# Cross-attention with its mask and its normalisation bias carried in the last row of the keys

## The chip, the core and the metric

The kernel runs on one core of a Trainium2 chip. The core has five engines that run their own instruction streams in program order: TensorE (PE, matmuls, with its weight loads shown apart as PEld), VectorE (DVE), ScalarE (ACT), GpSimd (POOL) and SyncE (SP, which here only issues DMAs). They wait for each other through semaphores. The metric is the device time of one execution in microseconds (us), lower is better. Before the change it is 2433.44 us, the median of three runs from 2432.4 to 2435.29.

## What is computed

Four attention blocks follow each other on a batch of 8 sequences of 256 tokens with 128 features; a memory of 64 vectors with 64 features (`ctx_512`) feeds every cross-attention. Blocks L0, L1 and L3 have one layer each. Block L2 is six layers of a decoder, and takes most of the time:

```python
def step(t, p):                       # six times, with other weights
    tn = _ln(t, norm_g, norm_b)
    t = _mha(tn, tn, skv, sq, sow, sob, tgt_mask) + t      # self-attention, 256 x 256
    tn = _ln(t, norm_g, norm_b)
    t = _mha(src, tn, ckv, cq, cow, cob, src_mask) + t     # cross-attention, 256 x 64
    tn = _ln(t, pg, pb)
    t = t + (jax.nn.relu(tn @ w1 + b1) @ w2 + b2)

def _mha(s, t, kv_w, q_w, o_w, o_b, mask):                 # H = 16 heads of D = 64
    ...
    scores = jnp.einsum('bhqd,bhkd->bhqk', q, k) * D ** (-0.5)
    scores = jnp.where(mask[:, None] == 0, jnp.float32(-1000000000.0), scores)
    attn = jax.nn.softmax(scores, axis=-1)
```

`_ln` subtracts the mean of a token's 128 features, divides by the deviation, multiplies by `norm_g` and adds `norm_b`. The normalised features of a token therefore sum to zero before `norm_g` and `norm_b` come in. The change touches the cross-attention of these six layers, and the order of some steps that L0 shares with it.

## The kernel before

Everything stays on the chip between layers: `t` holds the 2048 tokens as 16 tiles of 128 tokens. A sequence `b` is two such tiles (`qt` = 0, 1). PSUM, where matmuls write, is one pool of four buffers (`two_banks`, tag "ps"), handed out in turn: a matmul that takes the fifth buffer in program order waits until the readers of the first are done.

The order of all work is written out by hand. `at(tick, phase, fn)` (L279) puts a step into a plan; at the end (L1271 to L1282) the steps are traced by tick and then by phase, and every compute engine is held to that order. SP is not. A tick is no fixed time, only a place in the order.

In a decoder layer, self-attention of sequence b begins at tick T0 + 4b, and its projections up to four ticks earlier. Cross-attention of sequence b begins at T_ca + 2b with T_ca = T0 + 32, so that one tick holds one tile of 128 tokens ("CA tile" 0 to 15 below); feed-forward of b follows seven ticks later; the next layer's self-attention projections begin at T_ca + 12. The last self-attention output steps of sequence 7 (`out_proj`, L966, and its addition into `t`, `add_out`, L977) stand at T_ca + 2, those of sequence 6 at T_ca - 2.

For cross-attention the query and key weights are multiplied together once per layer. `plan_ca_weights` (L1005) does so around tick T = T_ca - 6: `turned` and `fetched` transpose the weights by way of DRAM, `regrouped` (L1030, POOL, tick T + 1), then `folded("AT", ...)` (L1062, tick T + 2) makes the 1024 x 128 product `AT` and `folded("WVO", ...)` (L1063, tick T + 3) the product of value and output weights; each has 32 PE instructions and two ACT copies out of PSUM (L1052, L1054). `keys_both` (L1071, every fourth tick, at T_ca - 2, + 2, + 6, + 10) multiplies `AT` with the memory of two sequences, and four ACT copies (L1085) move the result out of PSUM as the keys.

The queries are the normalised tokens, made by `ahead` (L802): statistics on DVE (L808, L809), scale and shift per token on POOL (`scales`, L814 to L821), applied on ACT (L827), transposed on PE (L841), and multiplied by `norm_g` and shifted by `norm_b` per feature while ACT moves them out of PSUM (L843).

One CA tile then goes through the steps of `plan_weights_64` (L314), which L0 uses too:

- `scores`, tick n, phase 1, PE: 16 score matmuls of 128 x 32 by 128 x 256 (L341), and behind each four of them four bf16 matmuls of a 32-column `ones0` with the mask row (L348), which add -BIG to masked keys;
- `lower`, tick n, phase 2: ACT copies the scores to `e` (L357), DVE takes the maximum of each head (L359), POOL subtracts it (L360);
- `exps`, tick n, phase 8: ACT, exponential in place (L366);
- `divide`, tick n + 1, phase 2.4: DVE sums (L370) and inverts (L371), POOL multiplies (L372);
- `turn`, tick n + 2, phase 2.5: DVE transposes in blocks (L380);
- `sums`, tick n + 3, phase 3.0: PE multiplies with the values (L388), DVE adds the result into `t` (L1104).

So DVE's order in a tick is maximum of tile n, sum of tile n - 1, transposes of tile n - 2, and POOL's is subtraction of tile n, multiplication of tile n - 1. Behind them, in even ticks, come the statistics for one cross-attention and one feed-forward sequence (phase 6, DVE) and their `scales` (phase 8.4, POOL).

Of the kernel before, what the change touches and what calls it, by code (L numbers as in the profile page):

```python
# [27 lines left out]
def tile_xattn_stack(ctx: ExitStack, tc: tile.TileContext, io, out: bass.AP):  # L28
# [28 lines left out]
    def big(tag, bufs=4, shape=(P, 1024), dtype=F32):  # L57

        return heap.tile(list(shape), dtype, tag=tag, name=uniq(tag), bufs=bufs)
# [93 lines left out]

    norm_g = column("L2_norm_g")
    norm_b = column("L2_norm_b")
    pre_g = load_const("L2_pre_gT", [D, NL])
    pre_b = load_const("L2_pre_bT", [D, NL])
    ff_b1 = load_const("L2_ff_b1T", [P, NL, FF // P])
# [88 lines left out]
        return nm  # L247


    nm2 = const.tile([P, B, M], BF16, tag="nm2", name="nm2")  # L250
    nc.vector.memset(nm2, 0.0)
    ones0 = const.tile([P, 32], BF16, tag="ones0", name="ones0")
    nc.vector.memset(ones0, 0.0)
    nc.vector.memset(ones0[0:1], 1.0)


    def stats(xin, eps):
# [53 lines left out]
        )  # L311
        return vw

    def plan_weights_64(tick, qt, qT, keys, values, mask, take):  # L314

# [1 line left out]

        def scores():  # L320
            sc = two_banks("sc").rearrange("p (q x) -> p q x", q=4)
            if mask is None:
                for i in range(4):
                    for a in range(4):
                        q = (i + 2 * (a // 2)) % 4
                        rows = slice(64 * (a // 2), 64 * (a // 2) + 64)
                        qb = 4 * qt + q
                        nc.tensor.matmul(
                            sc[32 * a : 32 * a + 32, q, :],
                            lhsT=qT()[rows, qb * 32 : (qb + 1) * 32],  # L330
                            rhs=keys()[rows, 4 * (a % 2) : 4 * (a % 2) + 4, :].rearrange(
                                "p h k -> p (h k)"
                            ),
                            start=True, stop=True,
                        )
                tl["sc"] = sc.rearrange("p q x -> p (q x)")
                return
            for q in range(4):
                qb = 4 * qt + q
                for a in range(4):  # L340
                    nc.tensor.matmul(  # L341
                        sc[32 * a : 32 * a + 32, q, :],
                        lhsT=qT()[:, qb * 32 : (qb + 1) * 32],
                        rhs=keys()[:, a].rearrange("p h k -> p (h k)"),
                        start=True, stop=False,
                    )
                for a in range(4):
                    nc.tensor.matmul(  # L348
                        sc[32 * a : 32 * a + 32, q, :], lhsT=ones0, rhs=mask,
                        start=False, stop=True,  # L350
                    )
            tl["sc"] = sc.rearrange("p q x -> p (q x)")

# [21 lines left out]

        def turn():
            e = tl.pop("e").rearrange("p (q h) (k x) -> p (h k) q x", q=4, x=32)
            eT = big("k" if mask is None else "o", shape=(P, 8, 4, 32))
            for i in range(2):
                nc.vector.transpose(eT[:, 4 * i : 4 * i + 4], e[:, 4 * i : 4 * i + 4])  # L380
            tl["eT"] = eT
# [12 lines left out]
        at(tick, 1, scores)  # L394
        at(tick, 2, lower)
        at(tick, 8, exps)
        at(tick + 1, 2.4, divide)
        at(tick + 2, 2.5, turn)
        at(tick + 3, 3.0, sums)


# [210 lines left out]

    def mask_keys():
        mi = big("q", dtype=I32)
        mi = mi[0:1, : B * M].rearrange("p (b m) -> p b m", b=B)
        nc.sync.dma_start(out=mi, in_=io["mask_Bx1xS2_if1"].rearrange("b o m -> o b m"))
        nc.vector.tensor_scalar(nm2[0:1], mi, 0.0, -BIG, ALU.is_equal, ALU.mult)

    mask_bf = []

# [41 lines left out]
    def plan_l0(b, T):  # L662
# [68 lines left out]
        at(T + 2, 3.2, make_values)  # L731
        for qt in range(QT):
            plan_weights_64(
                T + qt, qt, lambda: st["q"], lambda: st["k"], lambda: st["VW"], None,
                lambda ps, qt=qt: add(qt, ps),
            )
        at(T + 4, 6, moments)
# [267 lines left out]
    def plan_ca_weights(l, T):  # L1005
# [54 lines left out]
            at(T - 4 + i, -0.5, lambda i=i: fetched(i))  # L1060
        at(T + 1, 8.05, regrouped)
        at(T + 2, 3.6, folded("AT", 0, lambda c: st[1][:, :, c, :], HD ** -0.5))  # L1062
        at(T + 3, 3.6, folded("WVO", 1, lambda c: W["ca", l][2][:, c, :]))  # L1063

    keys_of = {}

    def plan_ca(l, b, T):
# [3 lines left out]
        def keys_both():  # L1071

            res = [big("q", shape=(D, 4, 4, M)) for _ in range(2)]
            for g in range(2):
# [7 lines left out]
                            start=True, stop=True,  # L1082
                        )
                for i in range(2):
                    nc.scalar.copy(  # L1085
                        res[i][:, :, 2 * g : 2 * g + 2, :].rearrange("p a r k -> p r a k"),
                        ps[:, :, :, i * M : (i + 1) * M],
                    )
            keys_of[b], keys_of[b + 1] = res

# [3 lines left out]
        def res():  # L1094
            st["tb"] = residual(b, W["ca", l][3])

        ahead(b, (T - 4, 6), (T - 3, 2.95), (T - 2, 2.9), norm_g, norm_b, st)
        if b % 2 == 0:
            at(T - 2, 3.7, keys_both)
        at(T + 2, 3.2, make_values)  # L1100
# [5 lines left out]
        for qt in range(QT):  # L1106
            plan_weights_64(
                T + qt, qt, lambda: st["tT"], lambda: keys_of[b], lambda: st["VW"],
                nm2[:, b].unsqueeze(1).to_broadcast([P, 4, M]), lambda ps, qt=qt: add(qt, ps),
            )  # L1110

    def plan_ff(l, b, T, T_second, steps=None):
# [117 lines left out]
    for l in range(NL):  # L1230
        T_ca = T0 + 4 * B
        T_next = T_ca + 2 * B
        for b in range(B):
            plan_sa(l, b, T0 + 4 * b)
        plan_ca_weights(l, T_ca - 6)
        for b in range(B):
            plan_ca(l, b, T_ca + 2 * b)
            T_ff = T_ca + 2 * b + 7
# [101 lines left out]
```

## Time and profile before

The profiled execution took 2433.93 us in all, and its span, from the first to the last instruction, is 2431.9 us. All times below are from this one execution, counted from the span's start.

| engine | busy us | share of the span | instructions |
|---|---|---|---|
| PE matmuls | 2349.5 | 97% | 42411 |
| PE weight loads | 1741.0 | 72% | 42411 |
| DVE | 1836.6 | 76% | 5988 |
| ACT | 1719.9 | 71% | 4528 |
| POOL | 1450.3 | 60% | 2483 |

The matmul count is twice the program's for most lines, because an f32 matmul leaves two records. A matmul's record is longer than the time it keeps PE from the next one (the records of one line overlap), so busy time over a line tells how long something of it was under way, not what its removal would free. The six cross-attention stages start (first record of L341) at 399.9, 771.4, 1144.3, 1516.1, 1888.2 and 2259.4 us, about 372 us apart, and the sixteen score blocks of the first stage at 399.9, 402.6, 409.5, 418.8, 423.1, 428.6, 432.9, 445.2, 451.2, 457.0, 464.8, 473.7, 483.9, 495.0, 504.5 and 511.8 us.

The groups of the table by line that the change touches, with count, busy us over all, and mean ns of one: the mask matmuls L348, 1536, 112.8, 274; the score matmuls L341, 3072, 218.6, 384; the key copies L1085 on ACT, 96, 49.3, 599; the maximum L359, 112, 136.8, 1221; the sum L370, 112, 135.3, 1208; POOL's subtraction L360 and multiplication L372, 112 each, 213.1 and 213.0, 1903 and 1902.

### The profile page before, as it was taken

To read this page: it belongs to the slowest core of one execution; us is meant where nothing else is said; L and a number is where in the kernel's file an instruction comes from. 1 tells how busy PE (TensorE), PEld (TensorE's weight loads), DVE (VectorE), ACT (ScalarE), POOL (GpSimd) and SP (SyncE) were. 2 spreads that over 40 slices of the span, in tenths; PEclk is the share of its full clock that TensorE was granted. 3 is DMA by queue.
4 is the path that set the end of the run, shared out by engine and by line. 5 is a ranking of instruction groups with operands and counts; after the bars stand their busy time and mean duration, and the time that the engine had idled before them with its cause. 6 is when DMAs were issued, how large, how long until landed. Compare 5 with 4: busy or idle time off the path is not lost.

```text
span 2431.9 us, 99981 instructions
## 1 busy us (share of the span) xinstructions
PE 2349.5 (97%) x42411; PEld 1741.0 (72%) x42411; DVE 1836.6 (76%) x5988; ACT 1719.9 (71%) x4528; POOL 1450.3 (60%) x2483
## 2 busy tenths in 40 slices
PE   8999999999999999999999999999999999999997
PEld 4667777677777777777777777777777777777675
DVE  4778887667888667888667888667888667888674
ACT  4567777667777667777667778567778657778662
POOL 3754556755556755556765556765555765555774
PEclk9999999999999999999999999999999999999998
DMA  6000022001022001012000012000013000011000
GB/s 178 2 2 20 20 72 65 2 3 30 20 64 73 3 3 30 20 55 73 12 2 26 23 52 77 12 2 18 25 43 85 21 2 18 25 28 39 2 4 16
DMA packets 102833, 76.87 MB, mean 32 GB/s; under 512 B 8114, under 2 KB 96882, under 8 KB 102387
## 3 DMA queue, kind: packets, MB, share of 16 engines
q1 hardware_dynamic: 101794, 70.16, 10.4%
q8 instruction: 333, 5.46, 1.0%
q14 instruction: 114, 0.93, 0.1%
q10 hardware_dynamic: 592, 0.33, 0.1%
HBM read 62.07 MB, written 8.39 MB: 29 GB/s over the span
## 4 chain that ended last, share of the span: by engine, by line
PE 79%; DVE 7%; ACT 7%; POOL 5%; issue 2%; DMA 0%; SPq 0%; POOLq 0%; DVEq 0%; ACTq 0%
PE mm L861 14%; PE sc L898 14%; PE mm L953 13%; PE mm L971 7%; PE mm L880 7%; PE mm L388 5%; PE sc L341 4%; PE mm L1137 3%; PE mm L1120 3%; DVE m L359 2%; ACT e L357 2%; POOL e L360 2%; PE mm L303 1%; PE tp L841 1%; PE mm L1079 1%
## 5 line engine op out<-in xcount | busy, mean ns | idle before, releaser
L927 POOL TENSOR_SCALAR e<-e,rs 128x256 f32<-128x256 f32 x1536 | 703.1, 478 | 674.9 <-DVE rs L925 665.6
L917 ACT ACTIVATE e<-e,mn 128x256 f32<-128x256 f32 x1536 | 758.2, 495 | 133.7 <-DVE mn L912 129.4
L912 DVE CUSTOM_DVE_ANT_0 e<-sc,nm 128x256 f32<-128x256 f32 x1536 | 542.5, 419 | 108.8 <-PE sc L898 106.2
L937 DVE STREAM_TRANSPOSE eTc<-e 128x512 f32<-128x512 f32 x768 | 517.3, 695 | 62.9 <-POOL e L927 61.6
L898 PE MATMUL sc<-k,q 64*32 64x256 f32 x12288 | 378.3, 380 | 1.9 <-ACT q L867 0.9
L953 PE MATMUL mm<-eTc,v 32*64 32x256 f32 x12288 | 363.7, 378 | 5.7 <-ACT AT L1054 3.3
L953 PEld LDWEIGHTS mm<-eTc,v 32*64 32x64 f32 x12288 | 276.8, 131 | 89.1 <-issue 22.4
L360 POOL TENSOR_TENSOR e<-e,m 128x1024 f32<-128x1024 f32 x112 | 213.1, 1903 | 208.4 <-DVE m L359 208.4
L359 DVE TENSOR_REDUCE m<-sc 128x16 f32<-128x1024 f32 x112 | 136.8, 1221 | 263.8 <-ACT e L357 263.8
L898 PEld LDWEIGHTS sc<-k,q 64*32 64x32 f32 x12288 | 220.9, 106 | 123.3 <-issue 49.6
L917 ACT ACTIVATION_READ_ACCUMULATOR e<-e,mn 128x1 f32 x1536 | 287.2, 187 | 0.0
L341 PE MATMUL sc<-q,tT 128*32 128x256 f32 x3072 | 218.6, 384 | 2.3 <-DVE t L1104 2.3
L372 POOL TENSOR_TENSOR e<-e,r 128x1024 f32<-128x1024 f32 x112 | 213.0, 1902 | 1.2 <-DVE r L371 1.2
L388 PE MATMUL mm<-v,o 128*128 128x128 f32 x1536 | 199.3, 285 | 0.2 <-ACT v L309 0.2
L388 PEld LDWEIGHTS mm<-v,o 128*128 128x128 f32 x1536 | 185.6, 198 | 15.9 <-issue 8.1
L861 PE MATMUL mm<-tT,w_sk 128*128 128x256 f32 x768 | 189.1, 389 | 0.0
L971 PEld LDWEIGHTS mm<-w_sow,o 128*128 128x128 f32 x1536 | 175.1, 192 | 16.2 <-issue 12.3
L880 PE MATMUL mm<-w_sv,tT 128*32 128x256 f32 x3072 | 185.7, 382 | 0.0
L286 ACT COPY v<-mm 128x1024 f32<-128x1024 f32 x96 | 97.2, 1013 | 124.1 <-PE mm L880 123.5
L971 PE MATMUL mm<-w_sow,o 128*128 128x128 f32 x1536 | 183.4, 278 | 0.7 <-ACT WVO L1052 0.7
L861 PE MATMUL mm<-tT,w_sq 128*128 128x256 f32 x768 | 173.6, 379 | 0.0
L861 PEld LDWEIGHTS mm<-tT,w_sk 128*128 128x128 f32 x768 | 138.1, 190 | 44.1 <-issue 29.2
(212 smaller groups left out, 3551.0 us busy)
## 6 DMA issues: line engine op xcount, KB each, us to landing
nm<-mask_d SPq DMA_DIRECT2D x192, 128.0 KB
wd<-o SPq DMA_DIRECT2D x48, 128.0 KB
w_sk<-in_L_sa_kv_dram SPq DMA_DIRECT2D x6, 512.0 KB
w_sv<-in_L_sa_kv_dram SPq DMA_DIRECT2D x24, 128.0 KB
w_sq<-in_L_sa_q_dram SPq DMA_DIRECT2D x6, 512.0 KB
w_sow<-in_L_sa_ow_dram SPq DMA_DIRECT2D x6, 512.0 KB
w_ckv<-in_L_ca_kv_dram SPq DMA_DIRECT2D x12, 256.0 KB
w_cq<-in_L_ca_q_dram SPq DMA_DIRECT2D x6, 512.0 KB
```

The source lines that it names most:

```text
L341: nc.tensor.matmul(sc[32 * a : 32 * a + 32, q, :], lhsT=qT()[:, qb * 32 : (qb + 1) * 32], rhs=keys()[:, a].rearrange("p h k -> p (h k)"), ...
L360: nc.gpsimd.tensor_tensor(e, e, m.unsqueeze(2).to_broadcast([P, 16, M]), ALU.subtract)
L388: nc.tensor.matmul(ps[:, :D], lhsT=eT[:, s].rearrange("p q x -> p (q x)"), rhs=vw[:, r, k, g, :], start=(s == 0), stop=(s == 7),)
L861: nc.tensor.matmul(ps[:, i * S : (i + 1) * S], lhsT=w[:, c * P : (c + 1) * P], rhs=st["tT"], start=True, stop=True,)
L880: nc.tensor.matmul(ps[32 * a : 32 * a + 32, i, :], lhsT=st["tT"][:, kb * 32 : (kb + 1) * 32], rhs=sv[:, a].rearrange("p g x -> p (g x)"), ...
L898: nc.tensor.matmul(sc[32 * a : 32 * a + 32, r, j, :], lhsT=st["q"][g][rows, a, qb * 32 : (qb + 1) * 32], rhs=st["k"][g][rows, a, :], start ...
L912: nc.vector.tensor_tensor_reduce(e[:, i, :], sc4[:, i, :], st["nm"][:, 2 * jj + i % 2, :], -1.0, 3.0 * BIG, ALU.add, ALU.min, mn[:, i : i ...
L917: nc.scalar.activation(e[:, i, :], e[:, i, :], AF.Exp, scale=-1.0, bias=mn[:, i : i + 1], accum_out=rs[:, i : i + 1],)
L927: nc.gpsimd.tensor_scalar(e[:, i, :], e[:, i, :], rs[:, i : i + 1], 1.0, ALU.mult, ALU.mult)
L937: nc.vector.transpose(eT[:, r, :, 2 * jj : 2 * jj + 2, :], e[:, 2 * r : 2 * r + 2, :].rearrange("p j (k x) -> p k j x", x=32),)
L953: nc.tensor.matmul(ops[a // 2][r * HD : (r + 1) * HD, a % 2, :S], lhsT=st["v"][kb // 4][rows, kb % 4, (2 * g + r) * HD : (2 * g + r + 1) * ...
L971: nc.tensor.matmul(st["ps"][:, j * D : (j + 1) * D], lhsT=st["oT"][c // 4][:, c % 4, j * P : (j + 1) * P], rhs=sow[:, c, :], start=(c == 0 ...
```

## The change

The mask and the bias of the normalisation move into the last of the 128 rows of the keys.

- The queries: `ahead` in `plan_ca` now gets `last_off` and `last_on` in place of `norm_g` and `norm_b`. `last_off` is 1 except in feature 127, where it is 0; `last_on` is the opposite. So the transposed query has the plain normalised features 0 to 126 and a constant 1 as feature 127. Since the normalised features sum to zero, feature 127 is minus the sum of the others.
- The fold: after `AT` is made, five new steps in `plan_ca_weights` multiply it by `norm_b` and sum over the features (`meet_bias`, POOL, and `sum_bias`, one DVE reduction), multiply it by `norm_g` (`scale`, POOL), subtract its last column from all (`lose_last`, POOL), and write the sum into the last column (`put_bias`, POOL). The whole fold starts a tick earlier, at T_ca - 7.
- The keys: the four moves out of PSUM in `keys_both` become DVE additions of `nm2`, which now holds 0, and -BIG in partition 127 for a masked key. `nm2` is f32, and the mask's DMA fills all 128 partitions.
- The scores: the mask matmuls L348 and `ones0` are gone.
- The order: `divide` moves from phase 2.4 to 0.9 of its tick, and `turn` from 2.5 to 0.8 of its tick. So they stand in front of `lower` (phase 2) of the tile that shares the tick, on DVE and on POOL, and this in L0 as well.
- Two small DMAs at the start bring `norm_g` and `norm_b` to all partitions (`norm_rows`).

```diff
-    nm2 = const.tile([P, B, M], BF16, tag="nm2", name="nm2")
...
+    nm2 = const.tile([P, B, M], F32, tag="nm2", name="nm2")
+    last_on = ident[:, P - 1 : P]
+    last_off = const.tile([P, 1], F32, tag="last_off", name="last_off")
+    nc.vector.tensor_scalar(last_off, last_on, -1.0, 1.0, ALU.mult, ALU.add)
...
                         rhs=keys()[:, a].rearrange("p h k -> p (h k)"),
-                        start=True, stop=False,
-                    )
-                for a in range(4):
-                    nc.tensor.matmul(
-                        sc[32 * a : 32 * a + 32, q, :], lhsT=ones0, rhs=mask,
-                        start=False, stop=True,
+                        start=True, stop=True,
                     )
...
-        at(tick + 1, 2.4, divide)
-        at(tick + 2, 2.5, turn)
+        at(tick + 1, 0.9, divide)
+        at(tick + 2, 0.8, turn)
...
+        def meet_bias():
+            st["z"] = big("q", shape=(P, HC, D))
+            nc.gpsimd.tensor_tensor(st["z"], st["AT"], rows(1), ALU.mult)
+
+        def sum_bias():
+            st["add"] = sm([P, HC], "add")
+            nc.vector.tensor_reduce(st["add"], st.pop("z"), AX.X, ALU.add)
+
+        def scale():
+            nc.gpsimd.tensor_tensor(st["AT"], st["AT"], rows(0), ALU.mult)
+
+        def lose_last():
+            last = sm([P, HC], "last")
+            nc.gpsimd.tensor_copy(last, st["AT"][:, :, D - 1])
+            nc.gpsimd.tensor_tensor(
+                st["AT"], st["AT"], last.unsqueeze(2).to_broadcast([P, HC, D]), ALU.subtract
+            )
+
+        def put_bias():
+            nc.gpsimd.tensor_copy(st["AT"][:, :, D - 1], st.pop("add"))
+
+        at(T + 2, 8.05, meet_bias)
+        at(T + 3, 2.35, scale)
+        at(T + 3, 8.05, lose_last)
+        at(T + 3, 8.7, sum_bias)
+        at(T + 4, -0.1, put_bias)
...
                 for i in range(2):
-                    nc.scalar.copy(
+                    nc.vector.tensor_tensor(
                         res[i][:, :, 2 * g : 2 * g + 2, :].rearrange("p a r k -> p r a k"),
                         ps[:, :, :, i * M : (i + 1) * M],
+                        nm2[:, b + i].unsqueeze(1).unsqueeze(1).to_broadcast([P, 2, 4, M]),
+                        ALU.add,
                     )
...
-        ahead(b, (T - 4, 6), (T - 3, 2.95), (T - 2, 2.9), norm_g, norm_b, st)
+        ahead(b, (T - 4, 6), (T - 3, 2.95), (T - 2, 2.9), last_off, last_on, st)
...
-        plan_ca_weights(l, T_ca - 6)
+        plan_ca_weights(l, T_ca - 7)
```

More of the change, by code (lines that the diff above doesn't have):

```diff
@@ L155, in tile_xattn_stack @@
     norm_b = column("L2_norm_b")
+    norm_rows = const.tile([P, 2, D], F32, tag="norm_rows", name="norm_rows")
+    for i, name in enumerate(("L2_norm_g", "L2_norm_b")):
+        nc.sync.dma_start(out=norm_rows[:, i, :], in_=io[name].partition_broadcast(P))
     pre_g = load_const("L2_pre_gT", [D, NL])
@@ L247, in load_mask @@
         return nm
-    nm2 = const.tile([P, B, M], BF16, tag="nm2", name="nm2")
[L251 to L254, printed above, removed]
+    nm2 = const.tile([P, B, M], F32, tag="nm2", name="nm2")
+    last_on = ident[:, P - 1 : P]
+    last_off = const.tile([P, 1], F32, tag="last_off", name="last_off")
+    nc.vector.tensor_scalar(last_off, last_on, -1.0, 1.0, ALU.mult, ALU.add)
+    last_big = const.tile([P, 1], F32, tag="last_big", name="last_big")
+    nc.vector.tensor_scalar(last_big, last_on, -BIG, None, ALU.mult)
     def stats(xin, eps):
@@ L312, in values_of, with plan_weights_64 @@
         return vw
-    def plan_weights_64(tick, qt, qT, keys, values, mask, take):
+    def plan_weights_64(tick, qt, qT, keys, values, halves, take):
         tl = {}
@@ L321, in scores @@
             sc = two_banks("sc").rearrange("p (q x) -> p q x", q=4)
-            if mask is None:
+            if halves:
                 for i in range(4):
@@ L377, in turn @@
             e = tl.pop("e").rearrange("p (q h) (k x) -> p (h k) q x", q=4, x=32)
-            eT = big("k" if mask is None else "o", shape=(P, 8, 4, 32))
+            eT = big("k" if halves else "o", shape=(P, 8, 4, 32))
             for i in range(2):
@@ L614, in mask_keys @@
         mi = big("q", dtype=I32)
-        mi = mi[0:1, : B * M].rearrange("p (b m) -> p b m", b=B)
-        nc.sync.dma_start(out=mi, in_=io["mask_Bx1xS2_if1"].rearrange("b o m -> o b m"))
-        nc.vector.tensor_scalar(nm2[0:1], mi, 0.0, -BIG, ALU.is_equal, ALU.mult)
+        mi = mi[:, : B * M].rearrange("p (b m) -> p b m", b=B)
+        nc.sync.dma_start(
+            out=mi, in_=io["mask_Bx1xS2_if1"].rearrange("b o m -> (b o) m").partition_broadcast(P)
+        )
+        nc.vector.tensor_scalar(nm2, mi, 0.0, last_big, ALU.is_equal, ALU.mult)
     mask_bf = []
@@ L733, in plan_l0 @@
             plan_weights_64(
-                T + qt, qt, lambda: st["q"], lambda: st["k"], lambda: st["VW"], None,
+                T + qt, qt, lambda: st["q"], lambda: st["k"], lambda: st["VW"], True,
                 lambda ps, qt=qt: add(qt, ps),
@@ L1062, in plan_ca_weights, with rows @@
         at(T + 2, 3.6, folded("AT", 0, lambda c: st[1][:, :, c, :], HD ** -0.5))
+        def rows(i):
+            return norm_rows[:, i].unsqueeze(1).to_broadcast([P, HC, D])
+        def meet_bias():
[11 more added lines that the diff above has]
+                st["AT"], st["AT"], last.unsqueeze(2).to_broadcast([P, HC, D]), ALU.subtract
+            )
+        def put_bias():
[5 more added lines that the diff above has]
+        at(T + 4, -0.1, put_bias)
         at(T + 3, 3.6, folded("WVO", 1, lambda c: W["ca", l][2][:, c, :]))
@@ L1108, in plan_ca @@
                 T + qt, qt, lambda: st["tT"], lambda: keys_of[b], lambda: st["VW"],
-                nm2[:, b].unsqueeze(1).to_broadcast([P, 4, M]), lambda ps, qt=qt: add(qt, ps),
+                False, lambda ps, qt=qt: add(qt, ps),
             )
```

## The prediction

> **What bounds the kernel now.** I read the page's busy shares first, then the table by line, then the timeline inside one cross-attention stage (399.9 to 514 us), because the change works there, six times over.
>
> ```profile
> PE 2349.5 (97%) x42411; PEld 1741.0 (72%) x42411; DVE 1836.6 (76%) x5988; ACT 1719.9 (71%) x4528; POOL 1450.3 (60%) x2483
> ```
>
> PE looks like the bound, and nearly is: between 395 and 485 us the table of windows has it busy 84.23 of 90 us. What the mask matmuls cost it is not their row in the table by line (112.8 us), since records overlap. It is the distance that they put between the score groups:
>
> ```profile
> 409.50 0.64 PE L341 MATMUL sc<-q,tT 128*32 128x256 f32 x8
> ...
> 409.96 0.29 PE L348 MATMUL sc<-nm,ones 128*32 128x256 bf16 x4
> ...
> 410.07 0.61 PE L341 MATMUL sc<-q,tT 128*32 128x256 f32 x8
> ...
> 410.50 0.29 PE L348 MATMUL sc<-nm,ones 128*32 128x256 bf16 x4
> ...
> 410.61 0.61 PE L341 MATMUL sc<-q,tT 128*32 128x256 f32 x8
> ```
>
> A mask group holds PE from 410.50 to 410.61: 0.11 us.
>
> But a second bound lies just under PE, a ring through four in-order engines:
>
> ```profile
> 425.51 1.06 ACT L366 ACTIVATE e<-e 128x1024 f32<-128x1024 f32 x1 [2.50 <-POOL e L360]
> ...
> 426.48 0.99 ACT L357 COPY e<-sc 128x1024 f32<-128x1024 f32 x1
> ...
> 427.51 1.23 DVE L359 TENSOR_REDUCE m<-sc 128x16 f32<-128x1024 f32 x1 [1.27 <-ACT e L357]
> ...
> 428.65 1.21 DVE L370 TENSOR_REDUCE r<-e 128x16 f32<-128x1024 f32 x1
> 428.81 1.90 POOL L360 TENSOR_TENSOR e<-e,m 128x1024 f32<-128x1024 f32 x1 [1.47 <-DVE m L359]
> ...
> 429.89 0.25 DVE L371 RECIPROCAL r<-r 128x16 f32<-128x16 f32 x1
> ...
> 430.67 1.90 POOL L372 TENSOR_TENSOR e<-e,r 128x1024 f32<-128x1024 f32 x1
> ...
> 430.75 1.06 ACT L366 ACTIVATE e<-e 128x1024 f32<-128x1024 f32 x1 [0.96 <-POOL e L360]
> ```
>
> Exponential of one tile, copy of the next, its maximum, its subtraction, its exponential: from 425.51 to 430.75, 5.24 us. Sum, reciprocal and multiplication run beside the ring. No tile can come faster; over tiles 0 to 11 of this stage the exponentials start at 406.62 and 484.52, so the mean distance is 7.08 us.
>
> **Part 1, mask matmuls gone.** 96 tiles x 4 groups x 0.109 us = 41.7 us, 7.0 us per layer, wherever PE sets the pace.
>
> **Part 2, the new order.** Sum, reciprocal and multiplication of tile n now stand ahead of maximum and subtraction of tile n + 1, on DVE and POOL. So they enter the ring: exponential 1.06, sum 1.21, reciprocal 0.25, multiplication 1.90, subtraction 1.90, and about 0.25 of hand-overs (0.03 to 0.15 each where nothing queues, as at L0's last tile: exponential 145.90, multiplication's end 150.53) give 6.6 us. The copy and the maximum are hidden behind the multiplication. The ring grows by 1.35 us, though DVE waits less for copies (263.8 us in the list of waits).
>
> Then the same recurrence tick by tick. In an even tick POOL also has the residual (0.73) and two `scales` chains (433.35 to 436.61, say 3.1 without their gap): before the next exponential it needs 0.73 + 3.1 + 1.9 + 1.9 = 7.7 us (tiles 5 and 9). In a tick with `keys_both` DVE's additions of part 3 stand between the maximum and the next sum. For tile 7, counted from the end of maximum 6: values and the first keys on PE 2.2 (they need the PSUM buffer that this maximum frees), four additions 2.7, four pairs of statistics 1.75, transposes 1.25, sum and reciprocal 1.5, hand-over 0.15, multiplication and subtraction 3.8, in all 13.35, less the 2.7 at which exponential 6 started: 10.7. Tile 3 has one pair set less: 8.6. Tile 11 stays PE's.
>
> Periods of tiles 1 to 11, before: 5.24, 8.03, 5.62, 5.23, 7.76, 7.82, 7.20, 5.24, 8.88, 6.63, 10.25, sum 77.9. After: 6.6, 6.6, 8.6, 6.6, 7.7, 6.5, 10.7, 6.5, 7.7, 6.6, 10.3, sum 84.4. That is **+6.5 us**, and the 5.2 us of mask work of tiles 0 to 11 vanish inside it. From tile 12 on the next layer's projections keep PE full, and four tiles give 4 x 0.44 = -1.7. Net +4.8 per layer. Bounds: +1 if PE's lead absorbs most of the longer ring, +7 if none of tile 12 to 15 comes back.
>
> **Part 3, keys on DVE.** Four ACT copies (599 ns) become four DVE additions; nearest row L411, an f32 128x512 TENSOR_TENSOR from PSUM, 692 ns, so 2.7 us a call with their overlap. ACT's relief is real at tile 2 (its exponential waited for these copies) and is in the 6.6 above. The cost is what queues behind them on DVE: statistics, reciprocal, two transposes, and L978, the self-attention addition. L978 frees a PSUM buffer that PE wants at once:
>
> ```profile
> 417.98 2.05 ACT L1085 COPY q<-mm 128x512 f32<-128x512 f32 x4
> ...
> 418.35 0.41 DVE L978 TENSOR_TENSOR t<-mm,tb 128x256 f32<-128x256 f32 x1
> ...
> 418.81 0.16 PEld L341 LDWEIGHTS sc<-q,tT 128*32 128x32 f32 x8 [0.17 <-DVE t L978]
> ```
>
> At T_ca + 2 that pushes the score block to about 421.3, a stall of some 3 us that the recurrence holds. At T_ca - 2 it is not in it: L978 starts at 394.50; behind additions from 393.5 to 396.2, statistics 0.9, reciprocal 0.2 and transposes 1.6 it starts near 398.6, and the second self-attention score block, due at 395.4, waits 3.6 us. DVE has no room there: 6.51 of 7 us busy from 388 to 395. `sum_bias` adds 1.2 (row L370) two ticks earlier. Low end: 3.9 us of new DVE work less 1.2 of waits for PE that fall away, 2.7. High end 7, if the lateness adds up. I take **+4.5** per layer, near the stall that the timeline shows.
>
> **Part 4, the fold.** POOL's three 128x1024 passes (1.90 each, row L360) and two small copies, 6 us a layer, lie in self-attention, where POOL waits 665.6 us for L925; without that cover 6 us a layer. The tick earlier gives ACT two of its four fold copies (1.01 each) where it has room, and brings the others under PE's values a tick sooner; PE's waits of 0.76, 0.16 and 0.38 there may go and another of 1.8 come. Nothing net, -1 to +1. Its DMAs move a tick on SP, past one mask load, with DMA at 10% of its time: nothing. `norm_rows` puts two issues of about 0.5 us on SP before loads not needed before 118 us, and the wider mask DMA holds DVE for 0 to 3 us once: 0.5. The query's scale and bias are other operands of the same ACT instruction: nothing.
>
> **Part 5, the clock.** After a PE gap of 2.71 us the granted clock in the records is 0.5 for 3.41 us from 438.95:
>
> ```profile
> 430.90 2.05 PE L388 MATMUL mm<-v,o 128*128 128x128 f32 x16
> ...
> 437.96 0.93 PE L841 MATMUL tp<-ident,xn 128*128 128x128 f32 x4 [2.71 <-ACT xn L827]
> ...
> 438.73 3.42 PE L388 MATMUL mm<-v,o 128*128 128x128 f32 x16
> ```
>
> The Trainium skill ("TensorE: Matmul & The Clock Gate", Part 1) says that the gate closes after at least one idle window of about 3.4 us. By that rule my stalls of 3.0 to 3.6 us would mostly cost nothing more. By the row 2.7 us are enough, and a closed gate loses up to 1.7 us. I go by the row: four such stalls per layer instead of one, half of their price inside the ring's slack: **+1.5**, between 0 and 5.
>
> The skill's start page ("Trainium Kernel Development and Optimization", Performance Expectations) also warns that matmul busy time is a bad measure and weight-load busy the better one: here 72% against 97%. By it PE had a quarter to spare and removing matmuls would bring nothing; by the gaps in time it has 6%. I use the gaps: PE's 7.0 us would be worth having if nothing else lagged.
>
> **Sum.** Per layer 4.8 + 4.5 + 1.5 = 10.8, six layers 65. L0 uses the same ring for 16 tiles; from tile 2 to 12 its mean period is 6.95, three of its periods are 5.2 to 5.3, and each may grow by 1.3: +2, 0 to 5. With the 0.5 of part 4 this is +67 on a span of 2431.9, so 2499, and about 2 us around it (2433.93 against 2431.9). The median shown, 2433.44, is 0.5 below that execution: **2500 us**. Own range: low ends 1 + 2.7 + 0 - 1 per layer give +16, or 2450; high ends 7 + 7 + 5 with L0's 5 give +119, of which hardly all meet: 2545.
>
> **Rivals.** (a) PE keeps the pace: the ring's lengthening fits below PE's ticks and DVE's lateness in the queue. Then -41.7 and little else: 2392. For it: 97% busy, and a mean period of 7.08 above 6.6. Against: the mean mixes PE's long ticks with four periods under 6.6. It decides at one point: less its mask work PE could do a tile in 7.08 - 0.44 = 6.65, so exponentials 0 to 11 would have to come 6.65 us apart or closer, with hardly any tick longer than the bare ring. Chance 0.11. (b) Only the entry stall of part 3 shows, the ring being absorbed: 6 x (4.5 - 7.0) = -15, 2418. Chance 0.06. (c) The gains and the lags cancel: 2429 to 2438. Chance 0.03. (d) The forecast: 0.80. That the mask is not removed can be excluded: no L348 is left in the new order of PE.
>
> A measurement of this kernel tells about 0.2%, 5 us, from no change. Faster (a, b) 0.17, same 0.03, slower 0.80. The range for eight in ten takes my own range and reaches down through (b) and (c): 2412 to 2545.
>
> **What would show it.** In the profile after: distance of the exponentials at least 6.5 us in all of tiles 1 to 10, 84 us over tiles 0 to 11; POOL's subtraction directly behind its multiplication, and no longer waiting for the maximum; PE gaps of 3 us in front of the second self-attention score block at T_ca - 1 and of the score block at T_ca + 3, released by the addition into `t`, and others in front of the values, released by the maximum; PE's share down to 92 or 93%; stages about 383 us apart. If the stages come 366 us apart, rival (a) is right and the ring was slack. If they come some 375 apart with gaps at T_ca - 1 alone, part 2 was wrong.

## The result and the profile after

The changed kernel takes 2495.36 us (median of four runs, 2489.1 to 2499.24) against 2433.72 for the kernel before in the same rounds (2432.4 to 2435.29). The ratio is 1.0258, with a 95% interval of 1.0242 to 1.0273: 62 us slower. The profiled execution took 2489.1 us, its span is 2486.9 (before: 2431.9), its mean granted clock 0.98 (before 0.986).

From the page after: the engines' busy time with its share of the span, the shares of the chain that ended last, and the groups of the ring (busy, mean ns of one, and the idle time before them with what ended it).

```profile
PE 2334.0 (94%) x40875; PEld 1714.8 (69%) x40875; DVE 1916.5 (77%) x6089; ACT 1669.6 (67%) x4432; POOL 1492.3 (60%) x2513
...
PE 68%; DVE 14%; POOL 12%; ACT 4%; issue 2%; DMA 0%; SPq 0%; POOLq 0%; DVEq 0%; ACTq 0%
...
L373 POOL TENSOR_TENSOR e<-e,r 128x1024 f32<-128x1024 f32 x112 | 213.0, 1901 | 225.2 <-DVE r L372 216.5
...
L371 DVE TENSOR_REDUCE r<-e 128x16 f32<-128x1024 f32 x112 | 135.3, 1208 | 143.7 <-ACT e L367 143.7
L367 ACT ACTIVATE e<-e 128x1024 f32<-128x1024 f32 x112 | 118.3, 1056 | 160.1 <-POOL e L361 160.1
L361 POOL TENSOR_TENSOR e<-e,m 128x1024 f32<-128x1024 f32 x112 | 213.3, 1904 | 7.4 <-DVE m L360 7.4
```

The page before has, for the same chain and the same groups:

```profile
PE 79%; DVE 7%; ACT 7%; POOL 5%; issue 2%; DMA 0%; SPq 0%; POOLq 0%; DVEq 0%; ACTq 0%
...
L360 POOL TENSOR_TENSOR e<-e,m 128x1024 f32<-128x1024 f32 x112 | 213.1, 1903 | 208.4 <-DVE m L359 208.4
...
L372 POOL TENSOR_TENSOR e<-e,r 128x1024 f32<-128x1024 f32 x112 | 213.0, 1902 | 1.2 <-DVE r L371 1.2
```

PE lost 3 points of its share, and DVE and POOL have 26% of the last chain instead of 12%. The subtraction (L361) hardly waits any more: 7.4 us for 112 tiles, before 208.4. The wait has gone to the multiplication: 225.2 us, before 1.2. The subtraction stands behind the multiplication (L373), and that waits for the sum, which waits for the exponential, which waits for the subtraction. These four steps close the ring.

The timeline of after in the first cross-attention stage shows one turn of it (start, length, engine, line, operation, idle before it and what released it):

```profile
417.18 1.06 ACT L367 ACTIVATE e<-e 128x1024 f32<-128x1024 f32 x1 [2.89 <-POOL e L361]
418.14 0.99 ACT L358 COPY e<-sc 128x1024 f32<-128x1024 f32 x1
418.27 1.22 DVE L371 TENSOR_REDUCE r<-e 128x16 f32<-128x1024 f32 x1 [1.65 <-ACT e L367]
...
419.52 0.25 DVE L372 RECIPROCAL r<-r 128x16 f32<-128x16 f32 x1
419.69 1.16 DVE L360 TENSOR_REDUCE m<-sc 128x16 f32<-128x1024 f32 x1
419.92 1.90 POOL L373 TENSOR_TENSOR e<-e,r 128x1024 f32<-128x1024 f32 x1 [2.08 <-DVE r L372]
421.78 1.90 POOL L361 TENSOR_TENSOR e<-e,m 128x1024 f32<-128x1024 f32 x1
...
423.72 1.06 ACT L367 ACTIVATE e<-e 128x1024 f32<-128x1024 f32 x1 [2.18 <-POOL e L361]
```

From exponential to exponential it is 6.54 us. The copy (L358) lies beside the sum and the maximum (L360) beside the multiplication, and neither has a part in it. Over tiles 1 to 11 the distances are 6.55, 6.54, 7.99, 6.53, 7.76, 6.54, 8.78, 6.54, 7.76, 6.53, 10.62, in all 82.1 against 77.9.

The other place is the entry, the stretch from the last exponential of a stage to the first of the next, in which self-attention and the fold run. The timeline of after, just ahead of the first stage:

```profile
379.44 1.84 POOL L930 TENSOR_SCALAR e<-e,rs 128x256 f32<-128x256 f32 x4 [0.81 <-DVE rs L928]
380.27 2.04 ACT L1055 COPY WVO<-mm 64x1024 f32<-64x1024 f32 x2
381.24 2.35 POOL L1079 TENSOR_TENSOR AT<-AT,norm_rows 128x1024 f32<-128x1024 f32 x1
...
381.33 0.66 PE L956 MATMUL mm<-eTc,v 32*64 32x256 f32 x8 [1.25 <-ACT WVO L1055]
...
382.36 4.02 PE L956 MATMUL mm<-eTc,v 32*64 32x256 f32 x80 [0.37 <-ACT WVO L1055]
...
395.86 2.45 DVE L1118 TENSOR_TENSOR q<-mm,nm 128x512 f32<-128x512 f32 x4
...
400.29 0.39 DVE L981 TENSOR_TENSOR t<-mm,tb 128x256 f32<-128x256 f32 x1
...
400.73 3.68 PE L956 MATMUL mm<-eTc,v 32*64 32x256 f32 x120 [1.29 <-DVE t L981]
```

PE waits 1.25 and 0.37 us in front of the self-attention values for the two copies of the fold, and 1.29 us for the addition into `t`, which stands behind the four key additions. Before the change PE's gaps there were 0.76, 0.16 and 0.38:

```profile
375.33 1.96 PE L1042 MATMUL mm<-w_cq,o 64*64 64x128 f32 x32 [0.76 <-POOL o L1033]
...
379.34 0.66 PE L953 MATMUL mm<-eTc,v 32*64 32x256 f32 x8 [0.16 <-ACT AT L1054]
...
380.38 1.99 PE L953 MATMUL mm<-eTc,v 32*64 32x256 f32 x64 [0.38 <-ACT AT L1054]
```

To compare kernels I cut each layer at three exponentials (means of the five layers that a further stage follows, us; from the exponentials' starts in each trace, so of one execution each). The runs named here are the experiments of the next section:

| kernel | tiles 0 to 11 | tiles 11 to 15 | entry | layer |
|---|---|---|---|---|
| before | 77.9 | 38.7 | 255.3 | 371.9 |
| after | 82.2 | 38.2 | 262.0 | 382.4 |
| new_order_alone | 79.8 | 38.7 | 256.6 | 375.2 |
| turn_first_alone | 79.2 | 38.7 | 255.0 | 372.9 |
| old_order | 80.2 | 38.9 | 259.8 | 378.9 |
| keys_on_act | 78.9 | 37.3 | 260.6 | 376.8 |
| old_order_keys_on_act | 77.7 | 37.6 | 259.0 | 374.3 |
| no_mask_matmuls | 77.1 | 37.2 | 254.7 | 369.0 |
| fold_early_alone | 77.7 | 38.7 | 256.7 | 373.1 |
| mask_free_fold_early | 76.9 | 37.6 | 255.9 | 370.3 |
| fold_back | 77.0 | 37.5 | 257.4 | 371.9 |
| passes_behind_scales | 77.1 | 38.0 | 259.5 | 374.6 |
| two_passes_out | 77.0 | 37.6 | 257.2 | 371.7 |
| mask_by_pe_in_keys | 79.4 | 36.7 | 259.1 | 375.2 |

The change costs 10.5 us a layer: 4.3 in the tiles, 6.7 in the entry, and 0.5 come back in between. Five such layers are 52.5; the rest of the 55.0 by which the span grew is the first entry (first cross-attention exponential at 410.6 instead of 406.6) less a little at the end.

### The profile page after: what moved, and what is told of

Same layout as the page of the kernel before. It is cut to its first block, busy times and chain, and to the rows that moved or that the text cites. A ratio compares the mean times of both kernels' runs of the same rounds, so it can differ in the third digit from the quotient of the medians.

```text
span 2486.9 us, 97041 instructions
## 1 busy us (share of the span) xinstructions
PE 2334.0 (94%) x40875; PEld 1714.8 (69%) x40875; DVE 1916.5 (77%) x6089; ACT 1669.6 (67%) x4432; POOL 1492.3 (60%) x2513
## 4 chain that ended last, share of the span: by engine, by line
PE 68%; DVE 14%; POOL 12%; ACT 4%; issue 2%; DMA 0%; SPq 0%; POOLq 0%; DVEq 0%; ACTq 0%
PE mm L864 13%; PE sc L901 12%; PE mm L956 12%; PE mm L883 7%; PE mm L974 7%; PE mm L389 3%; POOL e L361 3%; POOL e L373 3%; PE mm L1172 3%; PE sc L347 3%; DVE e L915 2%; DVE q L1118 2%; PE mm L1155 2%; DVE r L371 2%; POOL e L930 2%
## 5 line engine op out<-in xcount | busy, mean ns | idle before, releaser
L930 POOL TENSOR_SCALAR e<-e,rs 128x256 f32<-128x256 f32 x1536 | 703.3, 478 | 638.9 <-DVE rs L928 629.7
L915 DVE CUSTOM_DVE_ANT_0 e<-sc,nm 128x256 f32<-128x256 f32 x1536 | 542.4, 419 | 105.1 <-PE sc L901 100.1
L956 PE MATMUL mm<-eTc,v 32*64 32x256 f32 x12288 | 374.4, 383 | 23.5 <-ACT WVO L1055 9.7
L956 PEld LDWEIGHTS mm<-eTc,v 32*64 32x64 f32 x12288 | 282.7, 133 | 111.8 <-issue 23.8
L373 POOL TENSOR_TENSOR e<-e,r 128x1024 f32<-128x1024 f32 x112 | 213.0, 1901 | 225.2 <-DVE r L372 216.5
L371 DVE TENSOR_REDUCE r<-e 128x16 f32<-128x1024 f32 x112 | 135.3, 1208 | 143.7 <-ACT e L367 143.7
L367 ACT ACTIVATE e<-e 128x1024 f32<-128x1024 f32 x112 | 118.3, 1056 | 160.1 <-POOL e L361 160.1
L361 POOL TENSOR_TENSOR e<-e,m 128x1024 f32<-128x1024 f32 x112 | 213.3, 1904 | 7.4 <-DVE m L360 7.4
L347 PE MATMUL sc<-q,tT 128*32 128x256 f32 x3072 | 199.0, 403 | 13.3 <-ACT tT L846 13.3
L974 PEld LDWEIGHTS mm<-w_sow,o 128*128 128x128 f32 x1536 | 178.2, 195 | 17.6 <-issue 12.3
```

The source lines that it names most:

```text
L361: nc.gpsimd.tensor_tensor(e, e, m.unsqueeze(2).to_broadcast([P, 16, M]), ALU.subtract)
L373: nc.gpsimd.tensor_tensor(tl["e"], tl["e"], r.unsqueeze(2).to_broadcast([P, 16, M]), ALU.mult)
L915: nc.vector.tensor_tensor_reduce(e[:, i, :], sc4[:, i, :], st["nm"][:, 2 * jj + i % 2, :], -1.0, 3.0 * BIG, ALU.add, ALU.min, mn[:, i : i ...
L930: nc.gpsimd.tensor_scalar(e[:, i, :], e[:, i, :], rs[:, i : i + 1], 1.0, ALU.mult, ALU.mult)
L956: nc.tensor.matmul(ops[a // 2][r * HD : (r + 1) * HD, a % 2, :S], lhsT=st["v"][kb // 4][rows, kb % 4, (2 * g + r) * HD : (2 * g + r + 1) * ...
L974: nc.tensor.matmul(st["ps"][:, j * D : (j + 1) * D], lhsT=st["oT"][c // 4][:, c % 4, j * P : (j + 1) * P], rhs=sow[:, c, :], start=(c == 0 ...
```

## The experiments

The ratios are against the kernel before, run beside each kernel; its medians lay between 2431.0 and 2433.6.

**Order and keys.** Three kernels take parts of the change back, one makes the new order alone.

```diff
 old_order: after with
-        at(tick + 1, 0.9, divide)
-        at(tick + 2, 0.8, turn)
+        at(tick + 1, 2.4, divide)
+        at(tick + 2, 2.5, turn)
 keys_on_act: after with
-                    nc.vector.tensor_tensor(
+                    nc.scalar.copy(
                         res[i]..., ps[:, :, :, i * M : (i + 1) * M],
-                        nm2[:, b + i]....to_broadcast([P, 2, 4, M]), ALU.add,
                     )
 old_order_keys_on_act: both
 new_order_alone: before with divide at 0.9 and turn at 0.8
```

> The changed kernel with divide and turn back at phases 2.4 and 2.5, all else kept. Theory (the ring): the exponentials come 5.2 us apart again wherever PE lets them, score block 12 of a stage starts about 80 us after block 0 instead of 87.9, and the time falls by 40 to 48 us, to 2447 to 2455. Rival (the additions on DVE and what queues behind them carry the loss, and the ring had slack): the time stays within 10 us of the changed kernel's, 2485 or more.

Measured: 2472.37 us, ratio 1.0159 (1.0142 to 1.0176). Undoing the order gives 23 us, between the two theories. The table shows why not more: with the additions on DVE even the old order takes 80.2 us for tiles 0 to 11.

> The changed kernel with the keys moved out of PSUM by four ACT copies again, as before the change; the addition of the mask row is left out. Theory (the ring): the distances of 6.5 and 7.7 us stay, only the ticks with keys lose about 2.5 us each and the entry into a stage 2 to 4, so the time falls by 4 to 7 us per layer, to 2453 to 2471. Rival (the additions on DVE carry the loss): nearly all of it goes, and PE's saving shows, 2395 to 2415.

Measured: 2462.48 us, 1.0123 (1.0108 to 1.0138): 33 us, as expected.

> Both undone: divide and turn at their old phases and the keys moved by ACT copies, the addition of the mask row left out; the mask matmuls stay away, the fold keeps its new steps and place. Theory: with ring and queue gone PE's 7.0 us per layer come back less about 1 us per layer at the fold, 2392 to 2402. Rival (the fold a tick earlier, or the clock, carries a large part): 2410 or more.

Measured: 2441.95 us, 1.0037 (1.0021 to 1.0054). With both undone the kernel should have been 30 to 40 us faster than before; it is 8 us slower. This miss raises the question that the runs on the mask matmuls and the fold answer: are the mask matmuls worth so little, or does something else eat them?

> The kernel before, with nothing changed but divide at phase 0.9 and turn at 0.8. Theory (the ring): exponentials 6.5 us apart or more, 7.7 where two chains of scales stand on POOL, 3 to 5 us per layer lost, 2450 to 2465. Rival (the ring has slack, and the new order frees DVE of its waits for the copies): within 5 us of the kernel before, or faster.

Measured: 2452.99 us, 1.008 (1.0064 to 1.0096), as expected. So far order and keys make up 53.4 us (2495.36 less 2441.95): 20.5 for the order by itself, 30.4 for the keys by themselves, 2.5 more together. The 2.5 is within the noise: the intervals of the ratios are 3 to 4 us to each side.

**What the mask matmuls are worth.**

```diff
 no_mask_matmuls: before with
-                        start=True, stop=False,
+                        start=True, stop=True,
                     )
-                for a in range(4):
-                    nc.tensor.matmul(
-                        sc[32 * a : 32 * a + 32, q, :], lhsT=ones0, rhs=mask,
-                        start=False, stop=True,
-                    )
```

> The kernel before with one thing taken away: the four mask matmuls of each of its 96 cross-attention tiles (the mask is left out of the scores; nothing else is changed). Theory (the ring through ACT, DVE and POOL sets the pace of tiles 0 to 11 of each stage, PE only that of tiles 12 to 15): the exponentials of tiles 0 to 11 keep their distances within 1 us over the stage, four tiles give 0.44 us each and a little is had at the edges, some 2.5 us per layer: 2416 to 2422. Rival (PE sets the pace of all tiles): 41.7 us less, 2392 or close to it.

Measured: 2413.62 us, 0.992 (0.9905 to 0.9935), 19.2 us less and a little below the expected range. That is under half of the 41.7 that the matmuls hold PE. The table says where: tiles 0 to 11, in which 11 x 0.44 = 4.8 us of PE's work are gone, give 0.8 (several distances stay as they were to the hundredth, 5.24 and 7.76 among them); tiles 11 to 15 give 1.5 of 1.8 in the mean (in three of the five stages all of it, 36.65 instead of 38.40; in the other two, with 37.89 and 38.29, a stretch in which the granted clock is 0.5 takes most of it back), the entry 0.6. PE is not what sets the pace of the first twelve tiles.

**The fold: its place and its new steps.** Four corners of a square, all with old order, ACT copies and no mask matmuls: the fold at T_ca - 6 or - 7, with or without the steps that bring gain and bias into `AT`. A fifth run moves the fold alone.

```diff
 fold_early_alone: before with
-        plan_ca_weights(l, T_ca - 6)
+        plan_ca_weights(l, T_ca - 7)
 mask_free_fold_early: no_mask_matmuls with the same edit
 fold_back: old_order_keys_on_act with
-        plan_ca_weights(l, T_ca - 7)
+        plan_ca_weights(l, T_ca - 6)
```

> The kernel before with one thing added: the fold of the cross-attention weights a tick earlier (T_ca - 7). No step of the bias is in it. Theory (the earlier tick puts the two ACT copies of WVO in front of PE's values, with a gap of 1.25 and 0.37 us, and a half-clock stretch behind it): 3 to 4 us per layer, 2450 to 2460. Rival (the place is free, and the POOL passes and the DVE sum that come with the change's fold are what costs): 2430 to 2438.

Measured: 2438.37 us, 1.0022 (1.001 to 1.0035). The tick costs 5.5 us, a quarter of what I had expected, and the rival was close.

> The kernel with old order and keys on ACT, with the fold put back to T_ca - 6 and all its added steps kept (mask row not added). Theory (the fold's tick costs 3 to 4 us per layer, its added steps nothing): 2416 to 2424. Rival (the added steps on POOL and DVE cost it): 2436 or more.

Measured: 2431.21 us, 0.9992 (0.9983 to 1.0002). Moving the fold back gives 10.7, not 20: between the theories.

> The kernel before without its mask matmuls (the mask is left out of the scores) and with the fold at T_ca - 7; none of the added steps of the bias. It is the fourth corner of a square: mask-free with neither 2413.62, with the added steps 2431.21, with both 2441.95. Theory (the added steps cost some 18 us wherever they stand, the earlier tick 5 to 11 us): 2418 to 2425. Rival (the earlier tick is most of it, the steps are hidden there): 2432 or more.

Measured: 2422.63 us, 0.9963 (0.9948 to 0.9978), as expected. The square is complete:

| | fold at T_ca - 6 | fold at T_ca - 7 |
|---|---|---|
| without the steps | 2413.62 | 2422.63 |
| with the steps | 2431.21 | 2441.95 |

The steps cost 17.6 in the old place and 19.3 in the new, the tick 9.0 and 10.7. The kernel before was up to 2.6 us faster in some of these rounds than in others; by the ratios the steps cost 17.5 and 18.0, the tick 10.5 and 10.9. So the place makes no difference to the steps that is clear of the noise. In the old place `put_bias` is also too late for the keys. From the timeline of fold_back:

```profile
1136.80 1.90 POOL L1084 TENSOR_TENSOR AT<-AT,last 128x1024 f32<-128x1024 f32 x1
1138.76 0.20 POOL L1089 COPY AT<-add 128x8 f32<-128x8 f32 x1
...
1139.01 2.06 PE L1112 MATMUL mm<-ctx,AT 64*128 64x128 f32 x32 [1.74 <-POOL AT L1089]
```

PE waits 1.74 us for POOL's last small copy. With the fold a tick earlier this gap is not there, but the steps cost no less. Why not, the timeline of old_order_keys_on_act shows:

```profile
1118.30 1.85 POOL L930 TENSOR_SCALAR e<-e,rs 128x256 f32<-128x256 f32 x4 [0.81 <-DVE rs L928]
...
1120.11 2.37 POOL L1079 TENSOR_TENSOR AT<-AT,norm_rows 128x1024 f32<-128x1024 f32 x1
...
1122.46 1.84 POOL L930 TENSOR_SCALAR e<-e,rs 128x256 f32<-128x256 f32 x4
1124.25 0.19 POOL L1083 COPY last<-AT 128x8 f32<-128x8 f32 x1
1124.53 1.90 POOL L1084 TENSOR_TENSOR AT<-AT,last 128x1024 f32<-128x1024 f32 x1
1126.50 0.23 POOL L817 TENSOR_SCALAR ve<-mv 128x2 f32<-128x2 f32 x1
...
1128.16 0.88 ACT L830 ACTIVATE xn<-t,nm,rstd 128x128 f32<-128x128 f32 x2 [1.68 <-POOL nm L824]
...
1128.70 0.71 PE L844 MATMUL tp<-ident,xn 128*128 128x128 f32 x2 [1.91 <-ACT xn L830]
```

and beside it mask_free_fold_early, which has the same fold without the steps (its line numbers are smaller by 8: L922 is the multiplication L930, L809 the first operation of `scales`, L822 the making of xn, L836 its transposition):

```profile
1121.50 3.65 POOL L922 TENSOR_SCALAR e<-e,rs 128x256 f32<-128x256 f32 x8 [5.63 <-DVE rs L920]
...
1125.24 0.22 POOL L809 TENSOR_SCALAR ve<-mv 128x2 f32<-128x2 f32 x1
...
1128.45 0.87 ACT L822 ACTIVATE xn<-t,nm,rstd 128x128 f32<-128x128 f32 x2
...
1129.93 0.44 PE L836 MATMUL tp<-ident,xn 128*128 128x128 f32 x2
```

Without the steps, eight multiplications of self-attention run in one piece and `scales` begins 3.74 us after their start. With them a pass of 2.37 us stands in the middle, another of 1.90 behind, and `scales` begins 8.20 us after it: ACT waits 1.68 us for it and PE 1.91.

**Is it that one wait?** One number puts the second pass behind `scales`.

```diff
 passes_behind_scales: old_order_keys_on_act with
-        at(T + 3, 8.05, lose_last)
+        at(T + 3, 8.5, lose_last)
```

> The kernel with old order and keys on ACT (fold at T_ca - 7, mask row not added), and one number changed: POOL's pass `lose_last` stands behind the next stage's `scales` in its tick (8.5 instead of 8.05). Theory (POOL's added passes make `scales` late, so xn comes late and PE waits 1.9 us for it at T_ca - 2, or loses the same in a half-clock stretch): that gap is gone, 6 x 1 to 2 us less than 2441.95: 2429 to 2437. Rival (the fold's cost is the two copies of WVO in front of PE's values, POOL only fills a wait): 2440 to 2445.

Measured: 2442.03 us, 1.0047 (1.003 to 1.0063). A miss: the time is unchanged. The rival's number is met, but not its reason, as the next run shows. The gap of 1.91 is gone, as planned. But the pass now stands in front of the next multiplications, as the timeline of this run shows:

```profile
1136.28 1.90 POOL L1084 TENSOR_TENSOR AT<-AT,last 128x1024 f32<-128x1024 f32 x1
...
1138.41 1.85 POOL L930 TENSOR_SCALAR e<-e,rs 128x256 f32<-128x256 f32 x4
...
1139.38 0.71 DVE L940 STREAM_TRANSPOSE eTc<-e 128x512 f32<-128x512 f32 x1 [2.63 <-POOL e L930]
...
1140.93 0.38 DVE L915 CUSTOM_DVE_ANT_0 e<-sc,nm 128x256 f32<-128x256 f32 x1
...
1142.51 1.16 PE L1112 MATMUL mm<-ctx,AT 64*128 64x128 f32 x16 [0.69 <-DVE mn L915]
```

DVE waits 2.63 us for the multiplication before it can transpose, its next maxima (L915) come late, they give PSUM back late, and PE waits 0.69 here and 0.92 a little further on for tT. The entry stays at 259.5 (259.0 before the edit). So it was not that wait alone; the pass needs room in POOL's queue, wherever it stands. The next run takes the passes away instead of moving one.

```diff
 two_passes_out: old_order_keys_on_act with
-        at(T + 3, 2.35, scale)
-        at(T + 3, 8.05, lose_last)
```

> The kernel with old order and keys on ACT (fold at T_ca - 7, mask row not added), without two of POOL's three passes: `scale` and `lose_last` (the gain of the norm and the taking out of the last row are left out of the keys); the first pass, DVE's sum and the last small copy stay. Theory (the passes stand in POOL's queue in front of the self-attention multiplications, whose transposes and next maximum hold PE back: it is POOL's 2.4 and 2.1 us, not the place's waits): most of the 19 us between 2441.95 and 2422.63 goes: 2423 to 2432. Rival (DVE's sum of 1.2 us in front of the maximum is the cause): 2437 or more.

Measured: 2429.5 us, 0.9985 (0.9978 to 0.9991), as expected: of the 19.3 us, 12.5 go with two POOL passes (by the ratios 12.7 of 18.0). The other 6.9 belong to what stays (the first pass of 2.4 us, DVE's sum of 1.18, the last copy); these were not told apart.

**Which half of the order.**

```diff
 turn_first_alone: before with
-        at(tick + 2, 2.5, turn)
+        at(tick + 2, 0.8, turn)
```

> The kernel before with half of the new order: only the transposes of the turn ahead of the maximum (0.8), the sum, reciprocal and multiplication where they were (2.4). Theory (the sum, the reciprocal and the multiplication are what lengthens the ring, the transposes stand in DVE's wait for the copy): 2428 to 2440. Rival (the transposes in front of the maximum are what costs): 2445 to 2455, as with both.

Measured: 2443.34 us, 1.0052 (1.003 to 1.0074): 10.5 us, between the theories. The transposes are not free. In the table they cost 1.3 in the tiles, of it 1.06 at one (tile 4's exponential comes 6.29 us after tile 3's, before 5.23), and nothing in the entry. That is 1.0 a layer, 6 us, not 10.5: the table's execution took 2439.7 us, and of the five (2438.15 to 2448.48) the longer ones have the lower granted clock, 0.987 down to 0.982. A tick with no other work in it stays at 5.23, against 6.54 with `divide` moved too.

**A version meant to beat both.** It keeps the old order and ACT's copies, has `lose_last` behind `scales`, and lets PE put the mask into the keys' last row, once per key bank instead of once per score group.

```diff
 mask_by_pe_in_keys: passes_behind_scales with
...
+                for r in range(2):
+                    nc.tensor.matmul(
+                        ps[:, r], lhsT=pick, rhs=nm2[:, b : b + 2, :]....to_broadcast([P, 4, 2 * M]),
+                        start=True, stop=False,
+                    )
                 for a in range(4):
                     ...
-                            start=True, stop=True,
+                            start=False, stop=a == 3,
```

(`nm2` is bf16 again, with the mask in one partition; `pick` is a constant that puts it into row 127. Neither is shown.)

> A version meant to beat both kernels: old order, keys copied by ACT, `lose_last` behind `scales`, fold at T_ca - 7, and the mask put into the last row of the keys by PE, as the first matmul of each key bank (two bf16 matmuls of 512 columns for each of the two banks pairs, four per call, two calls per layer). Theory: as passes_behind_scales and at most 4 x 0.25 us more for one call a layer where PE sets the pace: 2430 to 2443, equal to the kernel before within 0.5%. Rival (the added bias steps still cost more than the 19 us that the mask matmuls were worth): 2443 or more.

Measured: 2449.0 us, 1.0072 (1.005 to 1.0093). Its rival was right. (A layer has four such calls, not two.) The bias steps must come with any mask in the keys' last row, since only they make the query's last row constant; at 17.6 to 19.3 us they cost about what the mask matmuls were worth, 19.2, and the fold's tick stands on top. Against passes_behind_scales the median is 7 us higher, with intervals that overlap: the table has 2.3 a layer more in tiles 0 to 11, where the new matmuls stand ahead of the keys, and 1.3 less behind them, where this execution has no stretch at half clock. The same kernel with the fold at T_ca - 6 was not run; with the 10.7 us of fold_back taken off it would be near 2438, an estimate. None of these kernels beats the one before while it computes the same.

## Why the prediction was right, and where it was not

The total was close: 2500 predicted, 2495 measured, 10.8 us a layer against 10.5. It is a sum of parts of which one, the fold, was put at nothing, and others were too large.

- **The ring: right.** Bare ring (ticks with no other work in it) predicted 6.6, measured 6.53 to 6.55 six times; with two `scales` chains predicted 7.7, measured 7.76 twice (tile 5 took that before as well, so only tile 9, before 8.88, tests it); tile 11 as PE's, 10.3 predicted and 10.62 measured. It runs through three engines, ACT, DVE and POOL, not four. In L0, put at +2, tiles 2 to 12 take 71.6 us after and 69.6 before, 71.3 in new_order_alone and keys_on_act, 69.7 in old_order. Tiles 3 and 7 were too long: 8.6 and 10.7 predicted, 7.99 and 8.78 measured. The chain of 13.35 us for tile 7 began with "values and the first keys on PE 2.2 (they need the PSUM buffer that this maximum frees)". The keys do not wait for it:

```profile
448.52 1.16 DVE L360 TENSOR_REDUCE m<-sc 128x16 f32<-128x1024 f32 x1
...
449.50 2.06 PE L1112 MATMUL mm<-ctx,AT 64*128 64x128 f32 x32
...
450.71 2.48 DVE L1118 TENSOR_TENSOR q<-mm,nm 128x512 f32<-128x512 f32 x4 [0.85 <-PE mm L1112]
```

  In this stretch of after's timeline the keys begin while the maximum still runs, and the additions start 1.0 us after it, not 2.2. The sum over tiles 1 to 11 is 82.1 instead of 84.4.
- **The mask matmuls vanish inside the ring: shown.** no_mask_matmuls gives 0.8 us of 4.8 in those tiles. What came back was taken as 1.7 a layer; by itself the removal is worth 2.9 (371.9 less 369.0), part of it in the entry.
- **The keys on DVE: right in sum, wrong in place.** Predicted 4.5 a layer, mainly a stall of 3.6 us in the entry. Old order, with and without: 378.9 less 374.3 is 4.6, but 0.8 of it in the entry, 2.5 in tiles 0 to 11 and 1.3 behind them. The addition into `t` (L978, after the change L981) was late as predicted (400.29; predicted near 398.6, before 394.50), but held up the values by 1.29 us instead of the score block by 3.6. Of the 1.3 behind tile 11 a part is the clock: there old_order has a stretch at half clock in all five stages, old_order_keys_on_act in three.
- **The gap at T_ca + 3: there, with another cause.** It was to be released by the addition into `t`. After's timeline has 2.21 us (13.3 over the six stages), released by ACT's move of the queries, which stands behind exponential and copy on ACT:

```profile
431.71 1.06 ACT L367 ACTIVATE e<-e 128x1024 f32<-128x1024 f32 x1 [4.26 <-POOL e L361]
432.67 0.99 ACT L358 COPY e<-sc 128x1024 f32<-128x1024 f32 x1
...
433.56 0.57 ACT L846 ACTIVATE tT<-tp,ident,last_off 128x256 f32<-128x256 f32 x1
...
434.19 2.36 PE L347 MATMUL sc<-q,tT 128*32 128x256 f32 x20 [2.21 <-ACT tT L846]
```

  The other gaps that were to show, in front of the values and released by the maximum, came to 2.5 us in the whole run, and PE's share is 94%, not 92 or 93.
- **The fold: the step that failed.** It was put at "Nothing net, -1 to +1", because its POOL passes "lie in self-attention, where POOL waits 665.6 us for L925". It costs 5.3 us a layer: 4.0 for the steps (374.3 less 370.3) and 1.3 for the tick (370.3 less 369.0). The prediction had named 6 us a layer as the price of the POOL work without cover; two thirds of it were paid. Of the 4.0, 3.1 lie in the entry, where old_order_keys_on_act has a stretch at half clock in one layer of five and mask_free_fold_early in none, so the clock is not the cause there. The waits were there, but they are the ring of self-attention: POOL waits for a reciprocal and must then multiply at once, since DVE's transposes and next maxima follow. A pass starts when its own operand is there, and whatever part of it reaches into that moment is paid: that is the reading of the two timelines above, and two_passes_out bears it out for 12.5 of the 19.3 us. The passes with a gain or bias row also take 2.35 to 2.38 us, not 1.90. For the tick, PE's waits changed as forecast: 0.76, 0.16 and 0.38 went, 1.25 and 0.37 came. That is 0.3 more; what the rest of the 1.3 is stays open.
- **The clock: the stretches came, their price is only estimated.** Four stretches of 3.41 us at half clock were expected in a stage; after has them at 383.0, 434.2, 444.5 and 492.2, and between 200 and 2380 us it has 21, before 6. What one costs depends on where it lies. Where PE sets the pace it is 1.6 us: before's second stage has one more than its first, and its tiles 11 to 15 take 40.0 us instead of 38.4. The stretch at 492.2 can account for after taking 38.2 there when 36.7 is what no_mask_matmuls needs in its first three stages. In the entry of old_order_keys_on_act it is nothing: the first of the five entries has one and takes 258.97 us, as two of the four without (the others 258.98 and 259.28), and PE waits 4.3 us in it instead of 6.0. The stretch only used up waits. In after all five entries have one, so its price there cannot be told from this kernel alone.

  A mean price comes from executions of one kernel: the 65 of the kernel before in the experiments have medians of 2435.2 us at a clock of 0.985 (17 of them) and 2429.6 at 0.988 (9), 1.9 us per 0.001, and after's four have 10.1 us from 0.98 to 0.973, 1.4 per 0.001. One stretch is 0.0007 of the span, so 1.0 to 1.3 us. For 15 stretches more that makes 15 to 20 us of the 62, where the prediction had 9 (six times 1.5). This is an estimate: time and clock go together here, but a longer wait can also be what brings a stretch, so the cause is not shown by it.

Of the rivals, (a) needed distances of 6.65 or less with hardly any longer tick; five of the eleven are longer. (b), some 375 us between stages with gaps at T_ca - 1 alone, is out too: they come 381.6 to 383.2 apart. Why it still came out: by place, the tiles 0 to 11 were charged 2.2 too much (6.5; measured 4.3), those behind were credited 1.2 too much (1.7; measured 0.5), and the entry with the clock was put at 6.0 and took 6.7. In the entry the right sum has other parts than those predicted: the steps of the fold 3.1 (259.0 less 255.9), its tick 1.2, the new order 1.6 (260.6 less 259.0), the keys 0.8, both together 0.6 more, and 0.6 back from the mask. The fold's share stood where 3.6 us of the keys had been expected. That was luck, not working.

## What to carry to other kernels

An engine's idle time is not room for a new pass: ask what it waits for, and what must follow at once when that comes; a pass that can be moved behind one waiter will stand in front of the next. Before removing work from the busiest engine, compare the distance between its tiles with the smallest distance the ring of the other engines allows; where the two are close, only the tiles outside the ring pay the gain out. Moving an operation ahead of another in an in-order queue adds to the ring whatever it waits for, not only its own time.

## What the runs showed of the hardware

The clock. The Trainium skill ("TensorE: Matmul & The Clock Gate", Part 1) says that the gate closes after at least one idle window of about 3.4 us, in a window that runs free. The fourteen traces agree with the free-running window, but the window need not be idle throughout. In each trace every half-clock stretch begins on a grid of 3.413 us, and it goes with how much of the grid's last window PE was idle. Between 200 and 2380 us, at full clock, none of some 8600 windows in which PE was idle for less than 45% was followed by a half-clock stretch, 40 of the 77 between 45 and 60% were, and all of nearly 100 above. So two gaps of 1.25 and 0.37 us in one window closed it (47% idle, old_order_keys_on_act at 749.0), while the same two gaps in fold_early_alone, cut by the grid's edge, did not in its second entry (gaps from 754.2 and 756.1; 37% idle in the fuller window). Where PE sets the pace such a stretch costs 1.6 us (40.0 against 38.4 above).

A POOL pass over 128 x 1024 that multiplies by a row repeated eight times took 2.37 us; the one that subtracts one value per row of 128 took 1.90, like the subtraction in the softmax.
